# First layer: the number rows that the one-hot rows are compared with, laid out as three pieces with gaps

## The chip, the cores and the metric

The kernel runs on one core of a Trainium2 chip. The metric is device time in microseconds (us) of one execution. Engines are named as in the profile: PE (TensorE, with its weight loads PEld), DVE (VectorE), ACT (ScalarE), POOL (GpSimd), SP (SyncE, which issues DMAs).

## What is computed

A graph of 12,500 nodes with 256 values each and 200,000 edges (`src`, `dst`; sorted by `dst`) goes through one large block. Cut to what matters:

```python
xn = layernorm(x)
# three graph layers, then log_softmax
msg = h[src]; s = segment_sum(msg, dst); cnt = segment_sum(1, dst)
h = s / max(cnt, 1) @ Wl.T + bl + h @ Wr.T        # leaky_relu after layers 0 and 1
# linear attention over all nodes, from xn
x = x + gnn(xn, edges) + attention(xn)
# mixture of 8 experts, the best 2 of each token
x = x + moe(layernorm(x))
```

The change concerns the sum over edges of the first graph layer, and there a side task: counting edges for some of the target nodes.

## The kernel before

The nodes lie in 98 blocks of 128 (`P`). Edges are put into slots of 128 that belong to one block of targets each. For a slot, POOL issues an indirect DMA (`gather`, line 1402) that fetches the 128 source rows into one of 32 message buffers; DVE makes a 128x128 one-hot matrix of the targets, four slots in one instruction (`make_hots`, line 1394); PE multiplies the two and adds into an accumulator in PSUM (`product`, line 1422). When a block of targets has had its last slot, DVE divides its sum by the count and clears the accumulator (`take_up`, lines 1448 to 1458); a product that reuses that place waits for the clearing.

The order of each engine's instructions is written out by hand. In layers 0 and 1 one turn of the loop in `on_the_way_of` covers four slots: four gathers, a product, a stage of the linear algebra that runs beside (`stage`), one `make_hots`, any `take_up`, then three more products, and after each of these one or two steps of a side task. A gather may run up to 32 slots ahead of the product that frees its buffer. POOL has nothing else to do in the loop but gathers of two kinds.

The last `DENSE` = 6 blocks have so many edges that they don't go by slots. For them a matrix of counts (how many edges lead from this source to that target) is made in layer 0 and multiplied with the node table later (line 1351). The side task of layer 0 makes these counts (`all_counted`), for three pairs of blocks one after the other. `sorted_by_source` sorts a pair's edges by source: eight at a time with a search for the largest and a replacement (`max` and `match_replace`, lines 1155/1156 and 1189/1190), with 43 gathers between the two rounds of sorting (line 1165, tile `got_runs`). `counted` then goes through 33 groups of three source blocks. For each of a group's six or nine columns of edges, `make` has DVE compare a row of numbers with the column: 0 to 383 with the sources (`src_hot`, line 1232) and 0 to 255 with the targets (`dst_hot`, line 1234). PE multiplies the two one-hot matrices (`p_n`, line 1252, and a row of totals, `whole`, line 1256), ACT copies the counts out (line 1258) and SP stores them. `src_hot` and `dst_hot` have two buffers, so the one-hots of a group can be made while PE reads those of the group before. The counting of one pair runs beside the sorting of the next. In one step of `make` DVE makes three such pairs of one-hot rows.

Before all this a first part sorts out the edges; it uses an identity matrix (`ident`) that is made from the tile `diff`.

Of the kernel before, what the change touches and what calls it, by code (L numbers as in the profile page):

```python
# [42 lines left out]
BF = mybir.dt.bfloat16  # L43
I32 = mybir.dt.int32
U16 = mybir.dt.uint16
U32 = mybir.dt.uint32
AF = mybir.ActivationFunctionType
OP = mybir.AluOpType
# [7 lines left out]
P = 128  # L56
# [18 lines left out]
LAST = 1  # L75
DENSE = 2 * PAIRS
SPAN = 3
TILES = 2
REST = 2

# [6 lines left out]
def gps_kernel(ctx: ExitStack, tc: tile.TileContext, x, src, dst, wlr, bl, wq, wk, wv,  # L87
               w_out, b_out, rw, w1, b1, w2, b2, out):
    nc = tc.nc
# [31 lines left out]

    NBIN = (NB + SPAN - 1) // SPAN
    PARTS = P // NBIN
# [3 lines left out]
    def stretch(k):  # L127
# [6 lines left out]
        width = math.ceil((m1 + d1 - lo) / P)  # L134
        mean, run = width * SPAN * P / N, 1
        while True:
# [15 lines left out]
    consts = ctx.enter_context(tc.tile_pool(name="consts", bufs=1))  # L152
# [18 lines left out]
    def rows(t, b, n):  # L171

        return t[b * P:(b + n) * P, :].rearrange("(j p) d -> p j d", p=P)
# [13 lines left out]
                       ap=[[0, P], [D, t.shape[0]], [1, D]])  # L187


    diff = consts.tile([P, P], I32, name="diff")  # L190
    nc.gpsimd.iota(diff, pattern=[[1, P]], base=0, channel_multiplier=-1)
    ident = consts.tile([P, P], F32, name="ident")
    nc.vector.tensor_scalar(ident, diff, 0.0, None, op0=OP.is_equal)
    cols = consts.tile([P, P], F32, name="cols")
    nc.gpsimd.iota(cols, pattern=[[1, P]], base=0, channel_multiplier=0,
                   allow_small_or_imprecise_dtypes=True)
# [78 lines left out]
    with ExitStack() as first:  # L275
        sort = first.enter_context(tc.tile_pool(name="sort", bufs=1))
        work = first.enter_context(tc.tile_pool(name="work", bufs=2))
        psum = first.enter_context(tc.tile_pool(name="psum1", bufs=1, space=PSUM))

        def first_norm(b, n):  # L280
            xt = work.tile([P, G, D], F32, name="xt", bufs=8)
# [152 lines left out]
        for c in range(KC):  # L434
# [17 lines left out]
                                op0=OP.is_lt, op1=OP.add, accum_out=start_c[:NB + 1])  # L452
# [24 lines left out]
                                       op0=OP.mult, op1=OP.add)  # L477
# [7 lines left out]
        for s0 in range(0, NS, 512):  # L485
            n = min(512, NS - s0)
            nums = work.tile([NB, 512], F32, name="nums", bufs=1)
# [7 lines left out]
                                    op0=OP.min)  # L495
# [80 lines left out]
        for c in range(NC):  # L576
            past = work.tile([P, NB], F32, name="past_c")
            nc.vector.tensor_scalar(past, ends, slot_no[:, c:c + 1], None, op0=OP.is_le)
            of = work.tile([P, 2], F32, name="of")
# [4 lines left out]
                                           op0=OP.mult, op1=OP.add)  # L584
            nc.vector.tensor_scalar(of[:, 1:2], of[:, 1:2], shift[:, 0:1], float(E),
                                    op0=OP.add, op1=OP.min)
# [3 lines left out]
                                    op0=OP.mult, op1=OP.add)  # L590
# [7 lines left out]
                                    op0=OP.subtract)  # L598
# [529 lines left out]
    class Counts:  # L1128
# [89 lines left out]
        def counted(self, k, whole, inv):  # L1218


            source, target, is_one = self.tables.pop(k)
            self.sorting = False
            segs, half = source.shape[1] // ROWS, k % 2 * 2 * P
            hots = {}

            def make(g):
                src_hot = self.pool.tile([P, 9, SPAN * P], BF, name="src_hot", bufs=2)
                dst_hot = self.pool.tile([P, 9, 2 * P], BF, name="dst_hot", bufs=2)
                hots[g] = []
                for i in range(segs * PARTS):  # L1230
                    c = i // PARTS * ROWS + i % PARTS * NBIN + g
                    nc.vector.tensor_scalar(src_hot[:, i, :], self.nums, source[:, c:c + 1], None,  # L1232
                                            op0=OP.is_equal)
                    nc.vector.tensor_scalar(dst_hot[:, i, :], self.nums[:, :2 * P],
                                            target[:, c:c + 1], None, op0=OP.is_equal)
                    hots[g].append((src_hot[:, i, :], dst_hot[:, i, :], is_one[:, c:c + 1]))
                    if i % 3 == 2:
                        yield

            yield from make(0)  # L1240
            for g in range(NBIN):
                if g + 1 < NBIN:
                    yield from make(g + 1)
                n = min(SPAN, NB - g * SPAN)
                sb = self.pool.tile([P, SPAN, 2 * P], F32, name="counts_sb")
                mine = hots.pop(g)
                for t0 in range(0, n, 2):
                    m = min(2, n - t0)
                    p = self.psum.tile([P, 2, 2 * P], F32, name="p_n")
                    for t in range(m):  # L1250
                        for i, (s_hot, d_hot, _) in enumerate(mine):
                            nc.tensor.matmul(p[:, t, :], s_hot[:, (t0 + t) * P:(t0 + t + 1) * P],  # L1252
                                             d_hot, start=(i == 0), stop=(i == len(mine) - 1))
                    if t0 == 0:
                        for _, d_hot, one in mine:
                            nc.tensor.matmul(whole[0:1, half:half + 2 * P], one, d_hot,
                                             start=False, stop=True, skip_group_check=True)
                    nc.scalar.copy(sb[:, t0:t0 + m, :], p[:, :m, :])
                    yield
                nc.sync.dma_start(rows(counts[k], g * SPAN, n), sb[:, :n, :])  # L1260

            row = self.pool.tile([1, 2 * P], F32, name="row", tag="counts_sb")
            nc.scalar.copy(row, whole[0:1, half:half + 2 * P])
            yield
            yield
            p_t = self.psum.tile([P, 2], F32, name="p_t")
            for q in range(2):
                nc.tensor.transpose(p_t[:, 1 - q:2 - q], row[:, q * P:(q + 1) * P],
                                    ident[0:1, 0:1])
            yield  # L1270
            mine = inv[:, NB - 2 * k - 2:NB - 2 * k]
            nc.vector.tensor_scalar(mine, p_t, 1.0, None, op0=OP.max)
            nc.vector.reciprocal(mine, mine)
            nc.vector.memset(whole[0:1, half:half + 2 * P], 0.0)
            yield

        def all_counted(self, psum, whole, inv):

            self.psum, self.pool = psum, open_pool(self.making, "counting")
            nc.vector.memset(whole, 0.0)  # L1280
            self.nums = self.pool.tile([P, SPAN * P], U16, name="nums")
            nc.gpsimd.iota(self.nums, pattern=[[1, SPAN * P]], base=0, channel_multiplier=0)


            self.least = self.pool.tile([P, 1], F32, name="least")
            nc.gpsimd.iota(self.least, pattern=[[0, 1]], base=0, channel_multiplier=1,
                           allow_small_or_imprecise_dtypes=True)
            self.less = self.pool.tile([P, 1], F32, name="less")
            for c in range(PARTS - 1, 0, -1):
                nc.vector.tensor_scalar(self.less, self.least, float(c * NBIN), float(-NBIN),  # L1290
                                        op0=OP.is_ge, op1=OP.mult)
                if c == PARTS - 1:
                    total = self.pool.tile([P, 1], F32, name="total")
                    nc.vector.tensor_copy(total, self.less)
                else:
                    nc.vector.tensor_add(total, total, self.less)
            nc.vector.tensor_add(self.least, self.least, total)
            nc.vector.tensor_scalar(self.least, self.least, float(SPAN * P), float(SRC0),
                                    op0=OP.mult, op1=OP.add)
            nc.vector.tensor_scalar(self.less, self.least, -64.0, float(SRC0 - NONE),  # L1300
                                    op0=OP.mult, op1=OP.add)
            for _ in range(16):
                yield

            def all_sorted():

                pairs = [self.sorted_by_source(k) for k in range(PAIRS)]
                for k, steps in enumerate(pairs):
                    while self.stored == k:
                        next(steps)  # L1310
                        yield
                for _ in range(MSGS - FEW):
                    yield
                for k, steps in enumerate(pairs):
                    for _ in range(MSGS if k else 0):
                        yield
                    yield from steps

            sorting, k, counting = all_sorted(), 0, None
            while k < PAIRS:  # L1320
                next(sorting, None)
                if counting is None and k in self.tables:
                    counting = self.counted(k, whole, inv)
                if counting and next(counting, 0) == 0:
                    k, counting = k + 1, None
                yield
            self.making.close()

        def sums(self, layer, acc, take_up, pairs=PAIRS, tiles=TILES, bufs=4):

# [351 lines left out]
```

## Time and profile before

| | us |
|---|---|
| three runs | 5909.58, 5910.56, 5920.0 |
| median | 5910.56 |
| the profiled execution's own time | 5902.73 |
| its span in the profile | 5900.9 |
| layer 0's first and last gather | 184.6 and 2064.5 |
| first and last comparison of `make` | 678.0 and 1462.2 |

The profiled execution is 7.8 us below the median of the runs. The span is the time from the first to the last instruction of that execution. In the profile a line of a group of instructions reads: line, engine, operation, output <- input, size, x count, then the time in which the engine was busy with them, the mean duration of one in ns, and the idle time before them with what ended it.

### The profile page before, as it was taken

How to read it: one execution, taken by the hardware profiler on the slowest of the kernel's cores; microseconds unless marked ns; L12 is line 12 of the kernel's file. 1: busy time of each engine (PE TensorE's matmuls, PEld its weight loads, DVE VectorE, ACT ScalarE, POOL GpSimd, SP SyncE). 2: the span in 40 equal slices, each digit the busy share in tenths (PEclk: the TensorE clock that was granted, in tenths of full speed). 3: DMA queues.
4: the chain of work that ended last, by engine and by line, in shares of the span. 5: the costliest groups of instructions: out<-in, count | busy, mean ns of one | idle time of the engine just before them, and what ended most of it. 6: DMA issues, size and time to landing. Idle time of an engine off the chain costs nothing. (4 is left out here: it accounts for less than half of the span.)

```text
span 5900.9 us, 75160 instructions
## 1 busy us (share of the span) xinstructions
PE 5059.7 (86%) x23992; PEld 3732.8 (63%) x23992; DVE 2601.7 (44%) x7130; ACT 1059.6 (18%) x1970; POOL 4104.9 (70%) x4146
## 2 busy tenths in 40 slices
PE   1577888889999979888888776699999999999998
PEld 0456566566778756666666554366666666666667
DVE  6637867576222223333333212244444444444433
ACT  3111111112000011111000000123223322322333
POOL 0677778777777767777777777666666666666661
PEclk9998999999999999999999988699999999999999
DMA  6666444455888767676887654656656665656551
GB/s 199 200 196 193 132 118 137 135 156 181 267 254 265 222 189 227 219 219 208 259 268 252 210 172 145 191 178 186 186 168 186 184 182 167 185 173 179 158 161 51
DMA packets 719939, 1114.50 MB, mean 189 GB/s; under 512 B 106304, under 2 KB 553046, under 8 KB 719308
## 3 DMA queue, kind: packets, MB, share of 16 engines
q0 software_dynamic: 213712, 604.20, 35.2%
q1 hardware_dynamic: 488271, 485.32, 25.3%
q10 hardware_dynamic: 17578, 20.04, 1.0%
q8 instruction: 224, 3.67, 0.3%
q14 instruction: 154, 1.26, 0.1%
HBM read 921.07 MB, written 188.11 MB: 188 GB/s over the span
## 5 line engine op out<-in xcount | busy, mean ns | idle before, releaser
L1402 POOL DMA_INDIRECT msg<-y,src_of x2480 | 2541.7, 1025 | 801.1 <-issue 675.8
L1402 POOL DMA_INDIRECT msg_parts<-y_parts,src_of x1404 | 1403.7, 1000 | 695.2 <-issue 346.3
L1422 PE MATMUL acc<-msg,hots 128*128 128x257 f32 (+1 forms) x4960 | 1398.6, 406 | 514.1 <-DMA msg<-y,src_of 286.9
L1422 PEld LDWEIGHTS acc<-msg,hots 128*128 128x128 f32 x4960 | 948.8, 201 | 788.4 <-issue 383.7
L1394 DVE TENSOR_TENSOR hots<-cols,dst_of 128x512 f32<-128x512 f32 (+1 forms) x971 | 664.3, 687 | 1058.8 <-PE acc L1422 1058.1
L994 PE MATMUL p_h<-turned,w_sb 128*128 128x512 f32 (+1 forms) x1728 | 753.7, 560 | 42.9 <-ACT hT L996 42.8
L963 PE MATMUL p_y<-w_sb,hT 128*128 128x256 f32 x3136 | 745.9, 381 | 4.2 <-DVE x L950 4.0
L1351 PE MATMUL whole<-y_c,count 128*128 128x256 f32 x2744 | 733.0, 391 | 9.3 <-issue 9.3
L1422 PE MATMUL acc<-msg_parts,hots 128*128 128x256 bf16 x4212 | 631.6, 277 | 31.5 <-DMA msg_parts<-y_parts,src_of 18.1
L1422 PEld LDWEIGHTS <-hots 128*128 128x128 bf16 x4212 | 415.3, 100 | 359.5 <-issue 257.9
L963 PEld LDWEIGHTS p_y<-w_sb,hT 128*128 128x128 f32 x3136 | 570.2, 191 | 73.9 <-DVE x L950 5.3
L1351 PEld LDWEIGHTS whole<-y_c,count 128*128 128x128 f32 x2744 | 533.5, 197 | 85.6 <-issue 9.7
L950 DVE SCALAR_TENSOR_TENSOR x<-p_y,comb,x 128x256 f32<-128x256 f32 x784 | 340.7, 476 | 443.6 <-PE p_y L963 443.4
L996 ACT ACTIVATE hT<-p_h,b_sb 128x512 f32<-128x512 f32 (+1 forms) x432 | 276.8, 647 | 1165.4 <-PE p_h L994 1156.6
L994 PEld LDWEIGHTS p_h<-turned,w_sb 128*128 128x128 f32 x1728 | 301.8, 193 | 231.7 <-issue 172.5
L664 ACT COPY turned<-p_tr 128x512 f32<-128x512 f32 (+1 forms) x270 | 137.7, 549 | 1655.3 <-PE p_tr L662 1535.0
L248 PE MATMUL p_mm<-wlr_sb,turned 128*128 128x512 f32 x784 | 361.5, 605 | 0.5 <-ACT turned L664 0.5
L258 DVE TENSOR_TENSOR yz<-p_mm,bl_sb 128x256 f32<-128x256 f32 x196 | 81.2, 423 | 504.6 <-ACT y L257 221.6
L1232 DVE TENSOR_SCALAR src_hot<-nums,source_of 128x384 bf16<-128x384 uint16 x693 | 224.4, 324 | 133.1 <-PE p_n L1252 132.9
L1252 PE MATMUL p_n<-dst_hot,src_hot 128*128 128x256 bf16 x2058 | 271.8, 283 | 0.4 <-DVE h L683 0.2
L248 PEld LDWEIGHTS p_mm<-wlr_sb,turned 128*128 128x128 f32 x784 | 152.7, 195 | 152.7 <-issue 136.6
L1252 PEld LDWEIGHTS <-src_hot 128*128 128x128 bf16 x2058 | 205.3, 101 | 59.7 <-issue 12.2
(301 smaller groups left out, 3838.6 us busy)
## 6 DMA issues: line engine op xcount, KB each, us to landing
count<-counts SPq DMA_DIRECT2D x294, 256.0 KB
y_c<-y SPq DMA_DIRECT2D x294, 256.0 KB
msg<-y,src_of POOLq DMA_INDIRECT x2480
counts<-counts_sb SPq DMA_DIRECT2D x96, 384.0 KB
h<-z SPq DMA_DIRECT2D x66, 512.0 KB
z<-yz SPq DMA_DIRECT2D x98, 256.0 KB
xT<-xT_tab SPq DMA_DIRECT2D x44, 512.0 KB
msg_parts<-y_parts,src_of POOLq DMA_INDIRECT x1404
```

The source lines that it names most:

```text
L248: nc.tensor.matmul(p, hT[:, k, j * P:(j + 1) * P], w[:, k, :], start=(k == 0), stop=(k == 1))
L664: nc.scalar.copy(tT[:, k, :n * P], p_tr[:, :n * P])
L950: nc.vector.scalar_tensor_tensor(xt[:, j, :], p[:, j - j0, :], comb[:, j, i:i + 1], xt[:, j, :], op0=OP.mult, op1=OP.add)
L963: nc.tensor.matmul(p[:, j - j0, :], hT[:, k, j * P:(j + 1) * P], e.w2[:, i, k, :], start=(k == 0), stop=(k == 1))
L994: nc.tensor.matmul(p_h[:, :n * P], e.w1[:, i, k, m * P:(m + 1) * P], tT[:, k, :n * P], start=(k == 0), stop=(k == 1))
L996: nc.scalar.activation(hT[:, m, :n * P], p_h[:, :n * P], AF.Gelu, bias=e.b1[:, i, m:m + 1])
L1232: nc.vector.tensor_scalar(src_hot[:, i, :], self.nums, source[:, c:c + 1], None, op0=OP.is_equal)
L1252: nc.tensor.matmul(p[:, t, :], s_hot[:, (t0 + t) * P:(t0 + t + 1) * P], d_hot, start=(i == 0), stop=(i == len(mine) - 1))
L1351: nc.tensor.matmul(acc[:, h * D:(h + 1) * D], c[:, j, h * P:(h + 1) * P], y[:, j, :], start=False, stop=True, skip_group_check=True)
L1394: nc.vector.tensor_tensor(hot[:, :n, :], cols.rearrange("p (o c) -> p o c", o=1).to_broadcast([P, n, P]), dst_of[:, s:s + n].rearrange("p ...
L1402: got = nc.gpsimd.indirect_dma_start(out=msgs[s % held] if e else msgs[s % held][:, :D], out_offset=None, in_=y_parts if e else y_tab[laye ...
L1422: got = nc.tensor.matmul(sums, hot, msgs[s % held][:, k * D:k * D + w], start=False, stop=True, skip_group_check=True)
```

## The change

The two rows of numbers are laid out differently. `nums` becomes three pieces of 128 numbers with a gap of two after each, together again 0 to 383. The targets get a row of their own, `nums_d`: three pieces of 86 numbers, 128 apart, together 0 to 257. The comparisons read the three pieces and write one run of 384 or 258 elements, as the compiled instructions show: input `[130, 3] [1, 128]`, output `[1, 384]`; input `[128, 3] [1, 86]`, output `[1, 258]`. The rows of `dst_hot` are two elements longer; PE reads the first 256, as before. Count and order of the comparisons stay. POOL has one more `iota`, for `nums_d`. `diff` moves from the pool that lives for the whole kernel to one of the first part, and its `iota` comes behind 98 small memsets on POOL.

```diff
+WIDE = 2 * P + 2
-    diff = consts.tile([P, P], I32, name="diff")
-    nc.gpsimd.iota(diff, pattern=[[1, P]], base=0, channel_multiplier=-1)
     ident = consts.tile([P, P], F32, name="ident")
-    nc.vector.tensor_scalar(ident, diff, 0.0, None, op0=OP.is_equal)
...
         psum = first.enter_context(tc.tile_pool(name="psum1", bufs=1, space=PSUM))
+        diff = sort.tile([P, P], I32, name="diff")
+        nc.gpsimd.iota(diff, pattern=[[1, P]], base=0, channel_multiplier=-1)
+        nc.vector.tensor_scalar(ident, diff, 0.0, None, op0=OP.is_equal)
...
-                dst_hot = self.pool.tile([P, 9, 2 * P], BF, name="dst_hot", bufs=2)
+                dst_hot = self.pool.tile([P, 9, WIDE], BF, name="dst_hot", bufs=2)
...
-                    nc.vector.tensor_scalar(src_hot[:, i, :], self.nums, source[:, c:c + 1], None,
-                                            op0=OP.is_equal)
-                    nc.vector.tensor_scalar(dst_hot[:, i, :], self.nums[:, :2 * P],
-                                            target[:, c:c + 1], None, op0=OP.is_equal)
-                    hots[g].append((src_hot[:, i, :], dst_hot[:, i, :], is_one[:, c:c + 1]))
+                    for hot, nums, of in ((src_hot, self.nums, source),
+                                          (dst_hot, self.nums_d, target)):
+                        nc.vector.tensor_scalar(
+                            hot[:, i, :].rearrange("p (a b) -> p a b", a=3), nums, of[:, c:c + 1],
+                            None, op0=OP.is_equal)
+                    hots[g].append((src_hot[:, i, :], dst_hot[:, i, :2 * P], is_one[:, c:c + 1]))
...
-            self.nums = self.pool.tile([P, SPAN * P], U16, name="nums")
-            nc.gpsimd.iota(self.nums, pattern=[[1, SPAN * P]], base=0, channel_multiplier=0)
+            nums = self.pool.tile([P, 3, P + 2], U16, name="nums")
+            self.nums = nums[:, :, :P]
+            nc.gpsimd.iota(nums, pattern=[[P, 3], [1, P + 2]], base=0, channel_multiplier=0)
+            nums_d = self.pool.tile([P, 3, P], U16, name="nums_d")
+            nc.gpsimd.iota(nums_d, pattern=[[WIDE // 3, 3], [1, P]], base=0, channel_multiplier=0)
+            self.nums_d = nums_d[:, :, :WIDE // 3]
```

## The prediction

> **What bounds the kernel now.** I read the busy times of the page first, then cut the span into stretches, then looked at the groups, the waits and the order of time inside the stretch in which the changed comparisons run (678 to 1470 us, in layer 0).
>
> ```profile
> PE 5059.7 (86%) x23992; PEld 3732.8 (63%) x23992; DVE 2601.7 (44%) x7130; ACT 1059.6 (18%) x1970; POOL 4104.9 (70%) x4146
> ...
> 678.00:840.00 162.00, 141.32 (x874) 104.11 (x873) 103.62 (x392) 23.06 (x50) 125.54 (x122) 0.96 0.43 124
> 840.00:1000.00 160.00, 134.34 (x838) 98.80 (x835) 136.44 (x420) 23.43 (x50) 130.75 (x97) 0.95 0.46 138
> 1000.00:1150.00 150.00, 125.45 (x714) 88.88 (x715) 83.36 (x310) 25.32 (x55) 116.29 (x113) 0.93 0.44 126
> 1150.00:1260.00 110.00, 90.12 (x524) 63.92 (x522) 91.53 (x269) 17.75 (x38) 89.88 (x67) 0.92 0.51 156
> 1260.00:1470.00 210.00, 193.53 (x1205) 141.67 (x1206) 135.44 (x501) 41.52 (x88) 161.87 (x159) 0.98 0.58 176
> 1470.00:2064.00 594.00, 562.22 (x2470) 460.18 (x2471) 140.42 (x284) 27.82 (x68) 446.30 (x452) 0.98 0.80 251
> ```
>
> After each stretch and its length stand the busy times of PE, PEld, DVE, ACT and POOL. DVE is busy 44% of the whole span, but 136 of 160 us in the second stretch and 92 of 110 in the fourth, where sorting (lines 1189, 1190) and comparing run together; I call them B and D, and the others A, C, E and F.
>
> ```profile
> L1402 POOL DMA_INDIRECT msg<-y,src_of x466 | 532.3, 1142 | 142.0 <-issue 132.9 <-DMA msg<-y,src_of 4.3 <-PE acc L1422 2.4
> L1232 DVE TENSOR_SCALAR src_hot<-nums,source_of 128x384 bf16<-128x384 uint16 x693 | 224.4, 324 | 133.1 <-PE p_n L1252 132.9
> L1234 DVE TENSOR_SCALAR dst_hot<-nums,target_of 128x256 bf16<-128x256 uint16 x693 | 198.1, 286 | 1.4 <-ACT target_of L1210 1.4
> L1165 POOL DMA_INDIRECT got_runs<-by_source,idx x86 | 91.3, 1061 | 26.0 <-issue 26.0
> ...
> POOL msg L1402 <- issue: 217.4, 714, 0.3
> POOL msg L1402 <- PE acc L1422: 7.8, 19, 2.3
> ...
> PE acc L1422 <- DVE inv_w L1448: 68.5, 36, 7.5
> PE acc L1422 <- DMA msg<-y,src_of: 31.1, 11, 4.2
> ```
>
> POOL is never held up from 192 to 1470 us but for 0.3 us of issue ahead of each gather and once 2.3 us (the fifth and sixth lines). So the gathers run at POOL's own pace, and a gather takes 1142 ns here, against 985 ns in 1600 to 1800 us, where no comparisons run. PE waited 31.1 us for gathers and 68.5 us for DVE to clear an accumulator (the last two). Why gathers are slow shows in the order of time:
>
> ```profile
> 937.15 0.94 POOL L1402 DMA_INDIRECT msg<-y,src_of  x1 [0.30 <-issue]
> 938.17 0.95 DVE L1190 MATCH_REPLACE8 got_runs<-packed,got_runs 99x774 f32<-99x774 f32 x1
> 938.40 3.12 POOL L1402 DMA_INDIRECT msg<-y,src_of  x1 [0.30 <-issue]
> 939.04 0.31 DVE L1232 TENSOR_SCALAR src_hot<-nums,source_of 128x384 bf16<-128x384 uint16 x1
> 939.27 0.28 DVE L1234 TENSOR_SCALAR dst_hot<-nums,target_of 128x256 bf16<-128x256 uint16 x1
> 941.71 0.68 DVE L1394 TENSOR_TENSOR hots<-cols,dst_of 128x512 f32<-128x512 f32 x1
> ```
>
> A gather that starts under a replacement and runs on into comparisons takes 3.12 us in place of 0.94. The comparisons delay POOL.
>
> **The change part by part.**
>
> *The comparison's rate.* By the medians, 384 elements take 311 ns and 256 take 277: 0.266 ns per element. No row has 16-bit numbers in three pieces written as one run. Lower bound of its rate: 0.266, as now. Upper: 1.13, the search's (774 elements 947 ns, 688 elements 850 ns). Between them lie the single-input rows whose operands aren't both dense 16-bit runs: line 1182, which writes 16-bit numbers with gaps, 599 and 543 ns for 774 and 688 (0.65), line 1177 624 and 578 (0.535). These are nearest, since one side with gaps is what they share; I take 0.535. Then `src_hot` costs 384 x 0.269 = 103 ns more and `dst_hot` 258 x 0.535 - 256 x 0.266 = 70 more. If POOL no longer interferes, the start-to-start time after a `src_hot` falls from its mean 243 to its median 229 ns: -14. A pair: +159, one comparison +0.08 us. All 1386 would be 110 us of DVE time. Ends: 0, and (384 + 256) x 0.864 / 2 = 0.28 us each.
>
> [...]
>
> *The gathers' delay.* An undisturbed gather takes 946 ns (median). The 552 gathers of the stretch lie 466 x 0.196 + 86 x 0.115 = 101 us above that. Sorted by what DVE ran beside them: comparisons alone 208 gathers, 11.5 us; with `make_hots` 67, 21.9; with a replacement 25, 35.1; with both 8, 15.8; no comparison 243, 16.9. Gathers beside `make_hots` alone still lie 0.163 above, beside it and a replacement 0.673; without comparisons I leave them that. So 11.5 + (21.9 - 10.9) + 35.1 + (15.8 - 5.4), less 5 for the rest's 0.026 each, is some 63 us: 4 in A, 32 in B, 3 in C, 20 in D, 4 in E. Bounds: 0 if the delay stays, 79 if all 552 go to the 985 ns of 1600 to 1800 us.
>
> *What of it reaches the end.* PE stays behind POOL by 4 slots (caught up, it waits) to 27 (POOL must wait for a buffer). At the gathers of 818.9, 1117.0 and 1251.7 us it is behind by 5, 4 and 6; at 1466.4 by 27. So POOL paces the work up to about 1268 us, and PE has little in hand only where it waits for gathers: 11.3 us in A, 1.5 in B, 11.2 in C, 0 in D up to 1260 on the path described next, 3.1 in E. What POOL wins past that stands still in message buffers.
>
> To see what paces PE when gathers are early, I went back through the trace from the product at 1894.8 us, always to what ended an instruction's wait, or else to the one before it on its engine; where PE waited for a gather I booked the wait and stayed on PE. Comparisons on this path: 29 in A, 180 in B, 96 in C, 132 in D, 56 in E. DVE gets into it by clearing accumulators late (22.4 us of PE's waits in B) and by the sorting ahead of `src_hot`; behind a longer comparison wait `take_up`, `make_hots` and the next search, and for those PE.
>
> The sum, on this path: A goes by POOL, -4 + 0.5 (the new `iota` at 192 us, like the 0.47 us of the old) = -3.5. B and C: 276 x 0.08 = +22.1, less the waits of 12.7: +9.4. D: 132 x 0.08 = +10.6. E: 56 x 0.08 - 3.1 = +1.4. Together **+18 us**. In E and F PE is busy 756 of 804 us and POOL at its buffer limit, so the shift passes on whole. Layers 1 and 2 keep their work.
>
> *The rest.* `diff`'s `iota` (0.23 us) comes behind 98 memsets of about 0.03 us; `ident` was made at 19.3 us, long after, and is first read at 89.5 us: 0, at most 2.9 if that cover were gone. The two more elements of `dst_hot` are in the 70 ns. PE's products keep 128x256: 0.
>
> On the profiled execution's 5902.7 this makes 5920.7; the runs' median stands 7.8 higher, so 5910.6 + 18 = **5928.6 us**.
>
> **The rivals.**
>
> *DVE's time is hidden, the gathers win.* DVE waits 132.9 us for PE ahead of `src_hot`; if the longer comparisons fall into these gaps, PE loses its waits for gathers, 27 us: 5884. Against it: in B and D DVE idles only 24 and 18 us, and 312 of the comparisons stand on the path. It decides below (3.5 + 12.7 + 3.1) / 0.08 = 241 comparisons on the path behind A; I count 464. Chance 0.20.
>
> *The two cancel, or the rate stays.* If gaps do not matter, neither comparison nor gather changes: 5911. The same comes out where some 240 comparisons count. For it: the pieces make long rows. Chance 0.25, a third of it for the rate staying.
>
> *One element at a time.* At 0.28 us each, 464 give 130 - 19 = +111: 6022; A and E would become DVE's too. Nothing but its bound speaks for it. Chance 0.05.
>
> *DVE binds* (forecast), 0.50. Its own range: at least +12; if all 1068 comparisons of B to E count, 85 - 19 = +66: 5923 to 5977.
>
> **How the numbers follow.** 0.2% is 12 us, about what a measurement can tell from no change. Faster 0.20, same 0.25, slower 0.50 + 0.05. The range holds 8 in 10 when it leaves out the slow rival, the top of the forecast's range and what may lie below the fast rival's 5884: 5882 to 5970.
>
> **What would show it.** Right: `src_hot` near 0.41 and `dst_hot` near 0.35 us; gathers under 1.05 us mean from 678 to 1470; B's DVE busy above 95%; PE's waits for gathers near 10 us and its waits for cleared accumulators above 68.5; layer 0's last gather some 18 us after 2064.5. Wrong: comparisons at 0.31 (rate kept); gathers still at 1.14 (another cause of the delay); or fewer waits on DVE than now and a shorter layer 0.

## The result and the profile after

Median of 12 runs 5924.2 us, of the kernel before 5910.4 in as many; the ratio is 1.0024, 95% interval 1.0014 to 1.0033. So the change costs 13.8 us (8 to 20), where 18 were forecast, and the time lies inside the stated range. The profiled execution of the changed kernel took 5933.5 us, the longest of its twelve.

The comparisons first, and the gathers of POOL in the same stretch (groups by shape, 678 to 1470 us, as shown before):

```profile
L1408 POOL DMA_INDIRECT msg<-y,src_of x460 | 455.0, 989 | 222.0 <-issue 123.0 <-PE acc L1428 91.4 <-DMA msg<-y,src_of 3.7
L1235 DVE TENSOR_SCALAR src_hot<-nums,source_of 128x384 bf16<-128x384 uint16 x683 | 274.9, 402 | 100.2 <-PE p_n L1254 100.1
L1235 DVE TENSOR_SCALAR dst_hot<-nums_d,target_of 128x258 bf16<-128x258 uint16 x684 | 231.3, 338 | 0.2 <-ACT target_of L1211 0.2
L1166 POOL DMA_INDIRECT got_runs<-by_source,idx x86 | 88.2, 1025 | 26.0 <-issue 25.3 <-DMA msg<-y,src_of 0.3 <-DVE yz L256 0.2
```

The mean comparison went from 324 to 402 ns and from 286 to 338. The gathers went the other way: 1142 to 989 ns and 1061 to 1025. Both halves of the change do what the forecast said. The idle time ahead of the gathers tells what became of the gain: 91.4 us of it now end with PE. The waits of POOL (192 to 1470 us) and of PE (678 to 1470 us):

```profile
POOL msg L1408 <- PE acc L1428: 93.8, 40, 11.3
...
PE acc L1428 <- DVE inv_w L1454: 99.2, 36, 10.4
PE acc L1428 <- DMA msg<-y,src_of: 5.0, 3, 3.6
```

POOL waited for PE 7.8 us before, now 93.8. PE waited 31.1 us for gathers, now 5.0, and 68.5 us for cleared accumulators, now 99.2. The pace passed from POOL to DVE and PE. The stretches (length, then busy PE, PEld, DVE, ACT, POOL):

```profile
678.00:840.00 162.00, 143.36 (x884) 104.67 (x884) 126.23 (x397) 23.55 (x50) 124.33 (x126) 0.96 0.45 127
840.00:1000.00 160.00, 129.40 (x780) 94.45 (x781) 146.43 (x395) 21.27 (x45) 94.52 (x97) 0.91 0.45 136
1150.00:1260.00 110.00, 86.34 (x486) 60.27 (x484) 92.87 (x255) 16.82 (x36) 72.48 (x74) 0.86 0.51 154
1260.00:1470.00 210.00, 189.69 (x1168) 137.59 (x1166) 165.35 (x503) 39.54 (x84) 145.83 (x146) 0.98 0.56 170
```

In the second stretch DVE went from 136.4 to 146.4 busy us while it finished less (395 instructions against 420), and POOL fell from 130.8 to 94.5. The place where a gather took 3.12 us looks like this now (order of time; the same sequence, a gather that starts at the end of a replacement):

```profile
907.79 0.95 DVE L1191 MATCH_REPLACE8 got_runs<-packed,got_runs 99x774 f32<-99x774 f32 x1
908.65 0.40 DVE L1235 TENSOR_SCALAR src_hot<-nums,source_of 128x384 bf16<-128x384 uint16 x1
908.70 0.94 POOL L1408 DMA_INDIRECT msg<-y,src_of  x1 [0.30 <-issue]
908.97 0.34 DVE L1235 TENSOR_SCALAR dst_hot<-nums_d,target_of 128x258 bf16<-128x258 uint16 x1
```

The gather runs beside comparisons and takes 0.94 us, the undisturbed time.

Where the time went, by the start of the same products of layer 0 in the two profiled executions:

| | before | after | difference | forecast up to there |
|---|---|---|---|---|
| product 384 (end of A) | 824.5 | 821.4 | -3.1 | -3.5 |
| product 544 (end of C) | 1123.4 | 1131.8 | +8.4 | +5.9 |
| product 640 (end of D) | 1284.2 | 1298.6 | +14.4 | +16.5 |
| product 784 (behind E) | 1507.9 | 1525.3 | +17.4 | +17.9 |
| end of layer 0's last gather | 2065.5 | 2082.9 | +17.4 | +17.9 |

The rest of the profiled difference of 30.8 us lies in layers 1 and 2, whose instructions are the same. From layer 0's last gather to the end, the profiles of this case taken on chips of this speed last between 3833 and 3849 us with equal work there, so I count it as scatter; the medians show 13.8.

The table compares one execution with one execution, so its single rows are less sure than they look. In the profile of the kernel with two pieces (first experiment below), whose comparisons and gathers run as before, product 544 starts at 1130.6 us, 640 at 1288.2, 784 at 1513.6, and the last gather ends at 2071.2: 4 to 7 us behind the profile before. And the waits are not all of the loss. From product 384 to product 784 PE does the same work in both profiles (3455 and 3454 matmuls) and takes 20.5 us longer after; 5.7 of these are longer busy time (585.1 and 590.8 us), at a mean granted clock of 0.94 before and 0.93 after. The forecast has no term for that, and whether the lower clock comes of the change is not shown.

### The profile page after: what moved, and what is told of

Its sections match the earlier page's. It is cut to its first block, busy times and chain, and to the rows that moved or that the text cites. A ratio compares the mean times of both kernels' runs of the same rounds, so it can differ in the third digit from the quotient of the medians.

```text
span 5931.7 us, 75158 instructions
## 1 busy us (share of the span) xinstructions
PE 5065.8 (85%) x23992; PEld 3733.2 (63%) x23992; DVE 2694.3 (45%) x7130; ACT 1059.6 (18%) x1970; POOL 4036.3 (68%) x4147
## 5 line engine op out<-in xcount | busy, mean ns | idle before, releaser
L1408 POOL DMA_INDIRECT msg<-y,src_of x2480 | 2475.9, 998 | 892.2 <-issue 669.7
L1235 DVE TENSOR_SCALAR src_hot<-nums,source_of 128x384 bf16<-128x384 uint16 x693 | 278.9, 402 | 101.6 <-PE p_n L1254 101.5
```

Of the source, the lines that this page charges most:

```text
L1235: nc.vector.tensor_scalar(hot[:, i, :].rearrange("p (a b) -> p a b", a=3), nums, of[:, c:c + 1], None, op0=OP.is_equal)
L1408: got = nc.gpsimd.indirect_dma_start(out=msgs[s % held] if e else msgs[s % held][:, :D], out_offset=None, in_=y_parts if e else y_tab[laye ...
```

## The experiments

Every ratio is against runs of the kernel before on the same chip. Two theories stood against each other. Mine: the comparisons take longer (medians 311 to 403 ns and 277 to 339) because the number of pieces is odd, and beside the longer ones the gathers are undisturbed, but early gathers help only as far as PE waited for them, and DVE's longer work stands on PE's path. The rival: the gathers' pace is what matters, so whatever frees them must show.

**Two pieces instead of three.** Gaps as before, but an even count.

```diff
-                            hot[:, i, :].rearrange("p (a b) -> p a b", a=3), nums, of[:, c:c + 1],
+                            hot[:, i, :].rearrange("p (a b) -> p a b", a=2), nums, of[:, c:c + 1],
...
-            nums = self.pool.tile([P, 3, P + 2], U16, name="nums")
+            nums = self.pool.tile([P, 2, 3 * P // 2 + 2], U16, name="nums")
...
```

> Both comparisons read two pieces with gaps (2 x 192 and 2 x 129) and write one run, so that the gaps are there but the outermost count is even. Theory (the odd number of pieces halves the rate, and the halved rate frees the gathers): 311 and 277 ns as in the kernel before, gathers of 678 to 1470 us at 1.14 us, time within 6 us of before (5910). Rival (gaps, or an input of several rows, slow the instruction): 403 and 339 ns as in the changed kernel, gathers at 0.99 us, 5924.

Measured: 5910.3 against 5906.1, ratio 1.0004 (0.9994 to 1.0013). What writes and reads the tiles, and the groups of 678 to 1470 us:

```profile
L1235 DVE TENSOR_SCALAR src_hot<-nums,source_of x693: 247/314/531, 674.4 to 1466.4; 128x384 bf16<-128x384 uint16 x174
L1235 DVE TENSOR_SCALAR dst_hot<-nums_d,target_of x693: 268/281/522, 675.8 to 1466.6; 128x258 bf16<-128x258 uint16 x174
...
L1410 POOL DMA_INDIRECT msg<-y,src_of x463 | 531.8, 1149 | 141.1 <-issue 131.0 <-DMA msg<-y,src_of 3.7 <-PE p_n L1254 3.7
```

Medians of 314 and 281 ns, and gathers as slow as before (1149 ns). Gaps alone change nothing; three pieces written as one run do (403 and 339 ns, gathers of 989). Whether that is because three is odd is not shown: no run has another odd number of pieces. From before to two pieces to three pieces, the rate and the gathers' delay change together. This kernel also has the moved `diff`, the second `iota` and the longer rows of `dst_hot`, so none of these costs time that can be measured.

**One comparison of the two.** Three pieces for the sources only (the edit shown), then for the targets only.

```diff
-                    for hot, nums, of in ((src_hot, self.nums, source),
-                                          (dst_hot, self.nums_d, target)):
...
+                    nc.vector.tensor_scalar(
+                        src_hot[:, i, :].rearrange("p (a b) -> p a b", a=3), self.nums,
+                        source[:, c:c + 1], None, op0=OP.is_equal)
+                    nc.vector.tensor_scalar(dst_hot[:, i, :2 * P], self.nums_d,
+                                            target[:, c:c + 1], None, op0=OP.is_equal)
...
```

> Only the comparison with the sources reads three pieces; that with the targets is a single run. Theory (DVE's time on PE's path sets the change): 232 comparisons on the path at +92 ns less 14 make +18 us, the gathers give back a part of 19 us, since the other comparison still delays them: between +3 and +15 us, 5913 to 5925, gathers between 1.02 and 1.10 us. Rival (the gathers' pace sets it): half of the delay gone and time below before by 10 us or more.

> Only the comparison with the targets reads three pieces. Theory: 232 on the path at +62 ns make +14 us, less a part of 19 us: between -3 and +12 us, 5907 to 5922, gathers between 1.02 and 1.10 us. Rival (the gathers' pace sets it): below before by 10 us or more.

Measured: sources only 5903.3 against 5906.1, ratio 1.0000 (0.9990 to 1.0010); targets only 5899.9, ratio 0.9988 (0.9977 to 1.0000). Both lie below the lower end of what I expected, and both gathers are faster than I expected: the groups of the two kernels, sources only and targets only,

```profile
L1407 POOL DMA_INDIRECT msg<-y,src_of x467 | 462.8, 991 | 210.5 <-issue 123.0 <-PE acc L1427 77.1 <-DMA msg<-y,src_of 4.9
```

```profile
L1407 POOL DMA_INDIRECT msg<-y,src_of x475 | 485.1, 1021 | 191.2 <-issue 125.5 <-PE acc L1427 54.5 <-DMA msg<-y,src_of 4.9
```

My expectation that half of the disturbing comparisons leave a good part of the delay was wrong. One longer instruction in a pair is enough to take away most of the delay (mean gather 991 and 1021 ns, against 1142 before and 989 with both longer). Sorted by what DVE ran beside them, gathers that met a replacement and then comparisons lay above 946 ns by 1.40 us each before (25 gathers, 35.1 us), by nothing with sources only (24) and by 0.49 us with targets only (28 gathers, 13.7 us). In the sources-only kernel the first instruction behind the replacement is already a longer one (407 ns on the mean), in the other only the second (338 ns).

With that the sums close. DVE's start-to-start time of a pair, means: 438 ns before, 574 changed, 518 sources only, 498 targets only. Times 232 pairs on the path, less the forecast's 19.2 us of waits: +12.4, -0.6 and -5.3 us. The medians moved by +13.8, -2.8 and -6.1 (for sources only the ratio, 1.0000, says 0).

**DVE's old time with free gathers.** The changed kernel with 198 of 693 pairs left out, and the kernel before with the same ones left out.

```diff
                 for i in range(segs * PARTS):
+                    if i in (2, 5, 8)[:segs] and segs == 2 or i in (4, 8) and segs == 3:
+                        hots[g].append(hots[g][-1])
+                        if i % 3 == 2:
+                            yield
+                        continue
```

> The changed kernel with 198 of its 693 pairs of comparisons left out (PE reads the pair before in their place, so the counts are not the reference's): DVE's time for comparisons is back at 495 x 0.58 = 287 us against 303 before, and the gathers stay undisturbed at 0.99 us. Theory (gathers that are early help only as far as PE waited for them): 15 to 30 us below before, 5880 to 5896. Rival (the gathers pace the layer, and DVE's added time hid their gain): the whole 60 us, 5850 or less.

> The kernel before with 198 of 693 pairs of comparisons left out, again; the counts are not the reference's. If the chip runs the kernel before near 5906 us: 10 to 25 us below before if gathers pace the work up to 1268 us (no more than the 27 us with three pieces and the same pairs left out), 40 us or more below if DVE's time alone counts. If it runs it near 6620 us: 30 to 45 us below, as in the first such run.

Measured: with pieces 5879.6 against 5906.1 (-26.5, ratio 0.9954, 0.9940 to 0.9967); with runs 5878.0 against 5906.3 (-28.3, ratio 0.9950, 0.9937 to 0.9963). Free gathers (996 ns on the mean) at about DVE's old load bring 26 us, not 60, so the gathers' pace alone is not what the layer's time follows. The 26 us agree with the forecast's limit, the 27 us that PE had waited for gathers on its path, but they do not show it. With pieces and pairs left out PE still waits 16.8 us for gathers (678 to 1470 us; 31.1 before):

```profile
PE acc L1433 <- DVE inv_w L1459: 66.2, 37, 7.0
PE acc L1433 <- DMA msg<-y,src_of: 16.8, 6, 4.9
```

So only some 14 us of these waits went. DVE's comparisons are some 20 us shorter in all than before (495 x 0.574 against 693 x 0.438), and how the rest of the 26 us divides is not shown. With runs, 70 us less DVE work than with pieces bought nothing more, since POOL paces there, with gathers of 1088 ns: PE waits 38.5 us for them (678 to 1470 us), more than before,

```profile
PE acc L1427 <- DVE inv_w L1453: 42.1, 35, 4.8
PE acc L1427 <- DMA msg<-y,src_of: 38.5, 12, 5.6
```

and POOL never more than 0.3 us for PE. The 28 us are 3 more than the 10 to 25 I gave it, and well short of the rival's 40.

**Pieces only beside the sorting**, where the forecast placed most of the loss.

```diff
+                    slow = self.packing
+                    if slow:
+                        src = src_hot[:, i, :SPAN * P]
+                        nc.vector.tensor_scalar(src.rearrange("p (a b) -> p a b", a=3), self.nums,
+                                                source[:, c:c + 1], None, op0=OP.is_equal)
...
+                    else:
+                        src = src_hot[:, i, :].rearrange("p (a b) -> p a b", a=3)[:, :, :P]
+                        nc.vector.tensor_scalar(src, self.nums, source[:, c:c + 1], None,
+                                                op0=OP.is_equal)
...
```

> Three pieces into one run only beside the second sorting (stretches B and D), again. If the chip runs the kernel before near 5906 us: 312 comparisons of the path at +0.078 us make +24, less 13 to 16 us of PE's waits for gathers: 5 to 15 us above before, product 544 of layer 0 later than before and PE's waits for gathers below 20 us. If early gathers in B and D were worth their price: 5 us or more below before. If the chip runs it near 6620 us: as in the first such run, some 16 us above.

Measured: 5913.8 against 5908.8, ratio 1.0008 (0.9999 to 1.0018), the lower end of what was expected; product 544 at 1125.8 us against 1123.4 before, a difference within the scatter of single profiles. PE's waits for gathers fell to half:

```profile
PE acc L1442 <- DVE inv_w L1468: 87.2, 36, 10.5
PE acc L1442 <- DMA msg<-y,src_of: 15.1, 4, 6.4
```

156 pairs of the path at 136 ns are 21 us. The 76 pairs of the path outside the sorting cost some 19 ns more each as well (458 ns from start to start, against 438), since the comparison with three pieces on both sides takes 346 ns and not the 311 that I had assumed for equal counts, a term that no run shows: 1.5 us. Less 16 of waits that makes +6 to +7; +5 was measured. The gathers are as good as undisturbed outside the sorting too (994 ns on the mean of the stretch). In those two stretches early gathers are not worth their price; the interval just reaches zero, so this stands on the sum and the waits as much as on the time.

**One comparison of six**: single runs, but the targets of a batch's first pair in three pieces.

```diff
+                    if i % 3 == 0:
+                        nc.vector.tensor_scalar(
+                            dst_hot[:, i, :].rearrange("p (a b) -> p a b", a=3), self.nums_d,
+                            target[:, c:c + 1], None, op0=OP.is_equal)
+                    else:
+                        nc.vector.tensor_scalar(dst_hot[:, i, :2 * P], self.nums[:, :2 * P],
+                                                target[:, c:c + 1], None, op0=OP.is_equal)
```

> The kernel with one comparison of six in three pieces a third time. If the chip runs the kernel before near 5906 us, as the prediction's did: gathers at 1.06 us or less and 8 to 18 us below before (a gather gets its turn at the first DVE instruction that leaves POOL alone), or gathers at 1.11 us or more and a time within 6 us of before (the delay goes with the time of the disturbing comparisons). If it runs it near 6620 us: no difference, as PE is then behind POOL throughout.

Measured: 5897.7 against 5906.3, ratio 0.9985 (0.9976 to 0.9993): 8.6 us below before, inside the 8 to 18 expected; the gathers, 1068 ns, just miss the 1.06 us or less that I expected with it. It is the lowest median of a kernel that computes everything, though too close to targets only (5899.9) to be told from it. What writes the tiles, the gathers, and PE's waits (678 to 1470 us):

```profile
L1240 DVE TENSOR_SCALAR dst_hot<-nums,target_of x462: 266/280/471, 679.2 to 1459.0; 128x256 bf16<-128x256 uint16 x154
L1236 DVE TENSOR_SCALAR dst_hot<-nums_d,target_of x231: 326/339/349, 678.7 to 1458.1; 128x258 bf16<-128x258 uint16 x116
```

```profile
L1411 POOL DMA_INDIRECT msg<-y,src_of x474 | 506.2, 1068 | 168.2 <-issue 131.1 <-PE acc L1431 28.6 <-DMA msg<-y,src_of 3.4
```

```profile
PE acc L1431 <- DVE inv_w L1457: 73.8, 36, 7.3
...
PE acc L1431 <- DMA msg<-y,src_of: 20.5, 7, 6.5
```

A third of the `dst_hot` run at 339 ns, the rest at 280. That takes 74 of the 196 ns off the mean gather (1142 to 1068) at a fifth of the DVE price (26 ns a pair against 136). The gathers that meet a replacement and then comparisons now lie 0.73 us above 946 ns each (24 gathers, 17.6 us), against 1.40 before. PE's waits for gathers fall by 10.6 us, a pair costs 26 ns more on the mean (232 pairs: +6.0), together -4.6; layer 0's last gather ends at 2061.0 us against 2065.5, and -8.6 was measured, with an interval of some -14 to -4. With the longer instruction first in a batch rather than second, the delay might go entirely, as with sources only; that was not tried.

**The same questions where PE is slower.** Other runs were made on chips on which the kernel before takes 6620 us: between 678 and 1470 us the granted clock is 0.85 to 0.87 in the profiles taken there, against 0.95 in the profile of the kernel before above. The kernels were: single runs with the same pairs left out; pieces beside the sorting; pieces everywhere else (the same edit with `slow = not self.packing`); and one of six, twice.

> The kernel before (single runs) with the same 198 of 693 pairs of comparisons left out, so that the counts are not the reference's: DVE's time for comparisons is 495 x 0.44 = 217 us, some 70 less than with three pieces and the same pairs left out. Theory (with single runs the gathers pace the work up to 1268 us, with pieces DVE and PE do): the gathers keep some 5/7 of their delay, 1.08 to 1.10 us each, and the time falls by 10 to 25 us below before, no more than with three pieces (27 below). Rival (DVE's time alone counts, early gathers are worth nothing): 40 us or more below before.

> Three pieces into one run only while the second sorting of a pair runs beside (stretches B and D); elsewhere the comparison with the sources reads three pieces and writes three pieces with gaps (both counts 3), that with the targets reads two pieces. Theory: the equal counts of 3 keep 311 ns; of the path's comparisons 312 get longer by 0.078 us, +24 us, and B's and D's delay of gathers (52 of 63 us) goes, of which PE can use 13 to 16: between +5 and +15 us against before. Rival (early gathers in B and D are what is worth having): 5 us or more below before.

> The reverse: three pieces into one run in stretches A, C and E only. Theory: B and D as before with their delay, 1.3 us a gather in B; A gains 3.5 us by its gathers, C and E have 152 comparisons of the path, +12 us, and 11 us of delay go: between -6 and +8 us. Rival (the added DVE time counts wherever it stands): +12 us or more.

> Single runs but for one comparison of six: that with the targets of the first pair of a batch of three reads three pieces. Theory of now (a gather that waits gets its turn at the first DVE instruction that leaves POOL alone, so one such instruction in a batch is enough): gathers at 1.06 us or less, 77 longer comparisons on the path, +4 us, less 12 to 19 us that PE no longer waits: 8 to 18 us below before. Rival (the delay goes with the time of the disturbing comparisons): gathers at 1.11 us or more and a time within 6 us of before.

> The kernel with one comparison of six in three pieces once more, on another chip than the last time, where PE and the transfers were so slow that the kernel before took 6620 us and POOL waited for PE all the time. If the gathers pace the work up to about 1268 us again: gathers at 1.06 us or less, 8 to 18 us below before. If the delay goes with the time of the disturbing comparisons: gathers at 1.11 us or more and a time within 6 us of before.

| | before | this | ratio (95%) |
|---|---|---|---|
| pairs left out, runs | 6619.9 | 6580.0 | 0.9941 (0.9919 to 0.9963) |
| pieces beside the sorting | 6619.9 | 6634.5 | 1.0026 (1.0001 to 1.0051) |
| pieces elsewhere | 6619.9 | 6636.1 | 1.0025 (1.0006 to 1.0044) |
| one of six | 6619.9 | 6612.5 | 0.9993 (0.9971 to 1.0014) |
| one of six, again | 6620.1 | 6626.7 | 1.0002 (0.9978 to 1.0027) |

The waits of POOL for a message buffer (192 to 1700 us) say why these are not the same experiments: pairs left out, pieces beside the sorting, one of six.

```profile
POOL msg L1407 <- PE acc L1427: 201.7, 81, 6.6
```

```profile
POOL msg L1422 <- PE acc L1442: 290.6, 90, 10.8
```

```profile
POOL msg L1411 <- PE acc L1431: 239.5, 81, 8.1
```

POOL waits there for PE 200 to 290 us, where it waited 19.3 in the same time on the chip of the forecast (7.8 of it up to 1470 us). From gather 384 to 800 PE is 15 to 30 slots behind POOL in these traces, 27 on the median, against 0 to 27 and 13 in the profile before. So an earlier gather is worth little there: one of six shows no difference twice, though the intervals leave room for up to 19 us either way. DVE's time counts in both directions: more of it costs 15 us in either half, and less of it gains 40, where the same kernel gained 28 on the faster chip.

The kernel with pieces elsewhere missed its expectation in another way as well, and the speed of the chip is not the reason. In stretches B and D it was to keep the gathers' delay, 1.3 us a gather in B. There it reads three pieces and writes three pieces for the sources, at 344 ns on the median, and two pieces for the targets:

```profile
L1246 DVE TENSOR_SCALAR src_hot<-nums,source_of x201: 274/344/509, 998.6 to 1452.0; 128x384 bf16<-128x384 uint16 x101
```

Its gathers in stretch B (998 to 1154 us here) take 1061 ns on the mean. On the same chip, in that stretch, single runs with pairs left out have gathers of 1315 ns, one of six 1183, and pieces beside the sorting 999. So this kernel did not put the delay back into B and D, and it is no test of what the delay there costs.

The expectations for these runs were made for the faster chip and their times do not hold here; three of them were repeated on it above. Pieces outside the sorting were not, so for the faster chip it is open what A, C and E cost by themselves; the table of products above gives -3.1 us for A and +3.0 for E, and C only together with B. What makes those chips slower stays open. The granted clock is lower there (above). That the transfers were slow as well, as the second expectation for one of six says, is not shown: the packets of queue q0 took 31.8% of 6623.6 us in that run against 35.2% of 5900.9 before, the same to within 2%.

## Why the prediction was right

The change of the median, +13.8 us, is 4.2 below the forecast's +18. It is at the edge of what I called measurable (12 us), and the interval of 8 to 20 reaches across it.

**The rate of the comparisons: right, with luck in the row it came from.** Forecast +103 and +70 ns; the medians rose by 92 (311 to 403) and 62 (277 to 339). That is 0.506 ns per element (92 / 384 + 0.266), and the forecast took 0.535 from line 1177. But its reason for that row was wrong: line 1177 reads and writes dense 32-bit numbers (99x774 f32 both ways), with no gaps on either side. The row that does have gaps on one side is line 1182, 0.65 ns per element; by it `src_hot` would have cost 147 ns more and `dst_hot` 100, against 92 and 62 measured. That the row came out near is luck. Two pieces with gaps kept the old rate (314 and 281 ns), so the pieces alone explain nothing. Why three pieces written as one run take longer is not shown.

**The mis-sized term: 0.08 us for each comparison on the path.** Measured from start to start, a pair went from 438 to 574 ns on the mean, +136 or 0.068 for one, where the forecast had +159. With that its own sum is 464 x 0.068 - 19.2 = +12.4, against +13.8 measured.

**The count of the path: right.** The same walk back through the trace after finds 479 comparisons behind A (174 in B, 101 in C, 127 in D, 77 in E), where 464 were forecast. The waits for gathers that it subtracted are gone from the path of B to E, and A gave back 3.1 of its 3.5 us. The landmarks agree to within 2.5 us at each point, though by stretches less well: B with C cost 11.5 where 9.4 were forecast, D 6.0 where 10.6 were. As the profiles of two kernels whose medians are equal (before and two pieces) lie 4 to 7 us apart from product 544 on, agreement as close as that is partly luck, and 5.7 us of what the table shows are PE's longer busy time, which the forecast did not count.

**The gathers' delay: gone, somewhat more than forecast, and worth no more for that.** The gathers of the stretch lay 101 us above 946 ns each and now lie 26.6 above; 75 went, 63 were forecast. Beside comparisons alone 289 gathers have 3.1 us left, beside a replacement 25 have none, beside `make_hots` 72 have 9.5. The limit of 27 us on what early gathers can bring is not shown, since no run reaches it by early gathers alone. Nothing speaks against it either: the best kernel that computes everything gained 8.6 us, the one with pieces and pairs left out 26.5.

**What would show it.** Gathers under 1.05 us: 0.989. PE's waits for gathers near 10: 5.0. Its waits for cleared accumulators above 68.5: 99.2. The last gather 18 us later: 17.4. Missed: DVE's busy share in B, above 95% by the forecast, is 91.5% (146.4 of 160). The work of B did not fit denser; it spread past 1000 us, with 395 instructions in the stretch against 420.

**The rivals.** That the gathers win needed fewer than 241 comparisons on the path; 479 are on it. That the rate stays is what two pieces gave (314 and 281 ns). One element at a time fell with 0.506 ns per element.

## What to carry to other kernels

Price a relief by what the next engine waited for it, not by how much faster the relieved engine gets, and follow the path again with that engine taken out: here PE's waits for gathers fell by 26 us when gathers got 75 us shorter, and the longer comparisons cost more. Where a sequence of DVE instructions delays another engine (here a gather took 3.12 us in place of 0.94), it can be enough to make one instruction in a batch a longer one, at the point where the other engine is caught: one comparison of six at 339 ns in place of 280 took the mean gather from 1142 to 1068 ns. And look which engine is behind on the chip in question: the same edit was worth 9 us on one and nothing that could be measured on another.

## What the runs showed of the hardware

**Where a gather is delayed.** Comparisons at 0.266 ns per element delay a gather by 0.055 us alone (11.5 us over 208 gathers). A gather that starts under a replacement and runs into such comparisons lies 1.40 us above 946 ns on the mean. With a slower comparison as the next instruction after the replacement that is nothing, as the second 0.49, as one in six 0.73. That a gather, once caught, waits for a longer instruction of DVE is a guess of mine from these numbers; what it waits for is not shown. Why the replacement is needed to catch it was not tried.

**Three pieces on both sides.** In the kernel with pieces only beside the sorting, the other comparisons read three pieces and write three pieces (by line; minimum, median and maximum):

```profile
L1246 DVE TENSOR_SCALAR src_hot<-nums,source_of x492: 274/346/1029, 676.0 to 1470.9; 128x384 bf16<-128x384 uint16 x164
L1238 DVE TENSOR_SCALAR src_hot<-nums,source_of x201: 341/404/414, 843.1 to 1252.4; 128x384 bf16<-128x384 uint16 x101
```

346 ns, between the 311 of a run and the 404 of pieces written as a run. Why it takes 35 ns more than a run is not shown. In the kernel with pieces elsewhere, where this form runs beside the sorting, the 22 gathers that start under a replacement and run into comparisons lie 0.27 us above 946 ns on the mean, against 1.40 before and 0.70 with one of six on the same chip. So a form that lengthens a pair by some 19 ns from start to start, against 136 for three pieces into one run, takes away most of the delay on that chip. A kernel that uses it throughout was not tried.

**Chips differ.** The same kernel takes 5906 us on some chips and 6620 us on others, and on the latter another engine sets the pace of layer 0: between 192 and 1700 us POOL waits 200 to 290 us for PE there, in three kernels, against 19.3 in the profile before.
